# A four-layer image network on one core: begin stages of the last layer let in earlier, measured durations for the list scheduler, one softplus table load, and an accumulation walked by rows

## The chip, the core and the metric

The kernel runs as one program on one core of a Trainium2 chip. The core has a matrix engine (PE, with its weight loads shown as PEld), a vector engine (DVE), a scalar engine for activation functions (ACT), a general engine (POOL) and an engine that issues DMA transfers (SP). Each works through its own queue in order, and they wait for each other on semaphores. The metric is the device time of the whole program in microseconds (us), lower is better.

## The reference

Four layers are applied to four images of 192 channels and 56 x 56 pixels, all in fp32: layer 0 is a windowed aggregation with a learned 7x7 kernel per pixel and an MLP; layer 1 scales channels by a frequency gate; layer 2 is overlapped window attention, a gated 3x3 depthwise convolution and an MLP with a second depthwise convolution; layer 3 is a selective scan in four directions. The change touches layers 2 and 3. Layer 3 in short:

```python
xn = layer_norm(x)                       # over channels
xc, z = split(in_proj @ xn)
u = silu(depthwise3x3(xc) + conv_b)
for k in (rows, columns, rows reversed, columns reversed):
    dt, B, C = split(x_proj[k] @ u)      # 12, 4 and 4 channels
    dt = softplus(dt_proj[k] @ dt + b[k])
    h[l] = exp(dt[l] * A) * h[l-1] + dt[l] * B[l] * u[l]   # 4 states per channel
    y += C[l] . h[l] + D[k] * u          # put back in pixel order
out = x + out_proj @ (layer_norm(y) * silu(z))
```

## The kernel before

The 192 channels lie as two halves of 96 partitions. An image is cut into 7 chunks of 448 pixels (8 rows of 56; for the column directions, 8 columns of 56).

**Who sets the order.** In layers 2 and 3 the order of the instructions on PE, DVE, ACT and POOL is made when the program is built, by a list scheduler (`Order`, L241 to L321). Each piece of work is a Python generator that yields, before an instruction, its engine, an estimated duration and the buffers it takes (`on_pe`, `on_dve`, `on_act`, `on_pool`, `on_sp`, L324 to L346), or a condition that must hold first (`yield lambda: ...`). Each generator is added with a *place*. At every step, among the first 130 generators by place, the one with the lowest estimated start plus 0.05 us per unit of place goes next. Estimated durations therefore decide the order, not only gates and places; they have no effect on the chip beyond that. `on_dve` bills 0.08 us plus 1.05 ns an element. When an activation needs another function table than the scheduler has noted, the scheduler emits a table load itself (L315). If the named set is not the one that the activation is built to use, the compiler adds another load before the activation.

**Layer 2** (L1077 to L1673). `dwconv` (L1333 to L1343) does both depthwise convolutions on DVE, nine taps of one instruction per part.

**Layer 3** (L1676 to L2139). The scan of one image has 28 steps: rows, columns, columns reversed, rows reversed, with 7 chunks each. A step `t` is done in two *half steps*, one per channel half, so an image has 56 and the layer 224. Places count half steps: `scan(t, h)` has place 2t+h. Its parts:

- `begin(b, c)` (L1792 to L1879), an image's first stages for one chunk: load of x (L1803), the channel norm (`layer_norm`, L1763 to L1790: matmuls at L1768 and L1783, DVE at L1770 and L1789), the input projection (L1821), the depthwise convolution as 18 matmuls with diagonal weights (L1851), activations into `u` and the gate, the store of the gate, and `product` for the row directions (L1893), whose result goes to DRAM (L1899).
- `begin_columns(b, c)` (L1881 to L1885): the same product with `u` read column by column; it needs the row stage of all seven chunks.
- `load` (L1954), `sizes` (L1975): bring a step's products back and make `dt` (PE at L1985, softplus on ACT at L1997), two steps at a time.
- `decay` (L2012): spreads `dt` over the states by DMA (L2023) and takes exponentials on ACT (L2031).
- `scan` (L2034): `du` on DVE (L2046, L2049), replication on PE (L2056), multiply by B and scan on DVE (L2062, L2078), multiply by C on POOL (L2085), sum over states on PE (L2101), and the addition into `y` on DVE (L2106 for the first direction, L2111 for the last, L2114 for the two column directions).
- `final(b, c)` (L1902 to L1947): output norm, gate, projection (L1929) and store.

Two `u` tensors exist, so images b and b+1 may be in work at once. When `begin(b, c)` may start is set by L1800 (a gate on `multiplied`, the count of half steps whose replication has been issued), and its rank against other work by its place (L2127); L2128 ranks the column products.

Of the kernel before, what the change touches and what calls it, by code (L numbers as in the profile page):

```python
# [21 lines left out]
HALF = 96  # L22
# [301 lines left out]
def on_pe(n, *takes, ready=None):  # L324

    return "PE", 0.0019 * n, takes, None, ready


def on_dve(*n, takes=(), ready=None):
    return "DVE", sum(0.08 + 0.00105 * i for i in n), takes, None, ready  # L330


def on_scan(n, ready):
# [7 lines left out]
def on_pool(*n, each=0.0011):  # L341
    return "POOL", sum(0.2 + each * i for i in n), (), None, None
# [4 lines left out]


EXP_LN, GELU = "natural_log_exp_and_others", "gelu_and_others"
SILU, SOFTPLUS = "silu_and_others", "softplus_and_others"  # L350


def layers01(tc, x_in, packs, aps, dst):
# [723 lines left out]
def layer2(tc, src, packs, aps, dst):  # L1077
# [12 lines left out]
    with ExitStack() as ctx:  # L1090
# [242 lines left out]
        def dwconv(parts):  # L1333


            for t in range(9):
                yield on_dve(*(n * W for _, _, _, n, _, _ in parts))
                for dst, pad, i, n, wt, bias in parts:
                    x = pad[:, i + t // 3 : i + t // 3 + n, t % 3 : t % 3 + W]
                    if t == 0:  # L1340
                        nc.vector.tensor_scalar(dst, x, wt[:, 0:1], bias, ALU.mult, ALU.add)
                    else:
                        nc.vector.scalar_tensor_tensor(dst, x, wt[:, t : t + 1], dst, ALU.mult, ALU.add)  # L1343
# [332 lines left out]
def layer3(tc, src, packs, aps, dst):  # L1676
# [8 lines left out]
    with ExitStack() as ctx:  # L1685
# [74 lines left out]
        def gone(*what):  # L1760
            return what in passed
# [30 lines left out]
        def begin(b, c):  # L1792
# [4 lines left out]
            yield lambda: (b, c) == (0, 0) or (gone("begun", b, c - 1) if c else gone("begun", b - 1, NCHUNK - 1))  # L1797
            yield lambda: b < 2 or gone("scanned", b - 2)

            yield lambda: b == 0 or gone("multiplied", 8 * NSC * (b - 1) + 6 * c)  # L1800
            yield on_sp("row", "row")
            xl, xn = take("row"), take("row")
            nc.sync.dma_start(xl[:HALF], pixels(src[b])[:, :, c * CH : (c + 1) * CH])  # L1803
# [71 lines left out]
            yield on_sp()  # L1875
            nc.sync.dma_start(pixels(zmem[b])[:, :, c * CH : (c + 1) * CH], zt)
            done(zt)
            yield from product(b, 0, px, u[:, :, px])
            passed.add(("rows", b, c))  # L1879

        def begin_columns(b, c):  # L1881
            yield lambda: all(gone("rows", b, i) for i in range(NCHUNK))
            uv = us[b % 2].rearrange("p h (y x) -> p h x y", x=W)[:, :, 8 * c : 8 * c + 8]
            yield from product(b, 1, slice(c * CH, (c + 1) * CH), uv)
            passed.add(("columns", b, c))  # L1885

        def product(b, o, px, u):

            n = px.stop - px.start
            yield on_pe(2 * n, "bank")  # L1890
            pp = take()
            for k in range(2):
                nc.tensor.matmul(pp[:40, :n], w["c128.xpT"][:, k, o], u[:, k], start=(k == 0), stop=(k == 1))  # L1893
            yield on_act(n, takes=("prod",))
            t = take("prod")
            nc.scalar.copy(t[:, :n], pp[:40, :n])
            done(pp)
            yield on_sp()
            nc.sync.dma_start(prods[b][o][:, px], t[:, :n])  # L1899
            done(t)  # L1900
# [133 lines left out]
        def scan(t, h):  # L2034
# [5 lines left out]
            px = slice(c * SCH, (c + 1) * SCH)  # L2040
            yield lambda: t in sized and (2 * t + h == 0 or gone("multiplied", 2 * t + h - 1))
            dts, b_, c_ = sized[t]
            yield on_dve(SCH, takes=("du",))
            du = take("du")
            if o == 0:
                nc.vector.tensor_mul(du, dts[h], u[:HALF, h, px])  # L2046
# [20 lines left out]
            for j in range(3):  # L2067
                g = 3 * h + j
                yield lambda: (t, h, j) in decays and (head or (t - 1, g) in states)
                da, at = decays.pop((t, h, j))  # L2070
                yield on_scan(SCH, ready=max(at, ends[j]))
                sts.append(take("st"))
                r = slice(None, None, -1 if s else 1)
                first = 0.0
                if not head:
                    before = states.pop((t - 1, g))
                    first = before[:, 0:1] if s else before[:, SCH - 1 : SCH]
                nc.vector.tensor_tensor_scan(  # L2078
                    sts[j][:, r], da[:, r], tiles[j][:, :SCH][:, r], first, ALU.mult, ALU.add
                )  # L2080
                done(tiles[j])
                if not head:
                    done(before)
                yield on_pool(SCH, each=0.0021)
                nc.gpsimd.tensor_mul(da, sts[j], c_)  # L2085
                das.append(da)
                if last:
                    done(sts[j])
                else:
                    states[t, g] = sts[j]  # L2090
# [14 lines left out]
            if (o, s) == (0, 0):  # L2105
                nc.vector.scalar_tensor_tensor(  # L2106
                    y[:HALF, h, px], u[:HALF, h, px], d_sum[:, h : h + 1], sums, ALU.mult, ALU.add
                )
                started.add((t, h))
            elif o == 0:  # L2110
                nc.vector.tensor_add(y[:HALF, h, px], y[:HALF, h, px], sums)  # L2111
            else:
                yv = y[:HALF, h].rearrange("p (y x) -> p x y", x=W)[:, 8 * c : 8 * c + 8]
                nc.vector.tensor_add(yv, yv, rows2(sums, H))  # L2114
            done(py)
            added[b] += 1
            if o == 0 and s == 1 and h == 1:
# [6 lines left out]
        n = 8 * NSC  # L2124
        for b in range(B):
            for c in range(NCHUNK):
                order.add(n * (b - 1) + 6 * c + 24, begin(b, c))  # L2127
                order.add(n * (b - 1) + 44 + c, begin_columns(b, c))  # L2128
                order.add(n * (b + 1) - 2 * c, final(b, c))
        for t in range(len(steps)):  # L2130
            order.add(2 * t - 5, load(t))
# [40 lines left out]
```

## Time and profile before

| | us |
|---|---|
| median of 3 runs (lowest to highest) | 7017.2 (7013.4 to 7018.1) |
| the profiled execution | 7014.4 |
| its span, first to last instruction | 7012.6 |
| layers 0 and 1 | 0 to 2969 |
| layer 2 | 2969 to 4909 |
| layer 3 | 4909 to 7013 |

| busy over the span | PE | DVE | ACT | POOL |
|---|---|---|---|---|
| us | 5931.5 | 5950.0 | 2699.1 | 1408.0 |
| share | 85% | 85% | 38% | 20% |

The layers' borders are the times at which the next layer's packed weights are fetched (L219). A group of instructions is shown as line, engine, operation, output<-inputs, shapes, count, then busy us and the mean ns of one, then the idle time of its engine just before and what ended most of it. PE's busy time is modelled and overlaps where small matmuls run side by side, so a share below 100% can be a full PE. A wait "X <- Y" means that X's engine stood idle until Y was done. In the tables by stretch of time, each engine has busy us and the number of instructions; then come the granted PE clock as a share of full speed, the share of DMA time and GB/s.

### The profile page before, as it was taken

Reading aid. Unit: us, or ns where it says so; the run is one execution under the profiler, and the core shown is the slowest. Engines: PE = TensorE matmul, PEld = TensorE weight load, DVE = VectorE, ACT = ScalarE, POOL = GpSimd, SP = SyncE. Lnnn points to the kernel's source line nnn. Section 1 sums busy time; section 2 is a strip of 40 time slices with the busy share of each in tenths; the row PEclk is TensorE's granted clock in tenths of the full one; section 3 lists DMA queues with packets and bytes.
Section 4 is the critical chain, followed back from the end, with each engine's and each line's share of the span. In section 5 each row is a group of like instructions: output and inputs, shape, how many; then the busy total and the mean of one; then the engine's idle time right before and its main releaser. Section 6 shows DMA issues by size and latency. Waiting matters only on the chain.

```text
span 7012.6 us, 107574 instructions
## 1 busy us (share of the span) xinstructions
PE 5931.5 (85%) x43810; PEld 2703.5 (39%) x43810; DVE 5950.0 (85%) x7379; ACT 2699.1 (38%) x4134; POOL 1408.0 (20%) x1409
## 2 busy tenths in 40 slices
PE   4999989999999994877888888875888999888856
PEld 2444444444544441344444454442322322222212
DVE  2799999999999999548999989997269779698697
ACT  1111111222212221144455555553356666566544
POOL 0000000000000000032222122210235445355354
PEclk9999989999999997989999999997999999999977
DMA  3222112221222112210000000000246555465454
GB/s 93 56 52 68 31 32 60 52 68 29 63 51 66 35 43 70 64 32 16 17 20 15 19 16 19 18 13 7 60 116 152 135 130 147 115 151 147 118 131 112
DMA packets 252043, 462.68 MB, mean 66 GB/s; under 512 B 30388, under 2 KB 237964, under 8 KB 240412
## 3 DMA queue, kind: packets, MB, share of 16 engines
q1 hardware_dynamic: 251548, 455.80, 25.6%
q8 instruction: 345, 5.65, 0.3%
q14 instruction: 150, 1.23, 0.1%
HBM read 238.58 MB, written 62.96 MB: 43 GB/s over the span
## 4 chain that ended last, share of the span: by engine, by line
DVE 47%; PE 36%; issue 7%; ACT 5%; POOL 2%; DMA 2%; SPq 0%; DVEq 0%; POOLq 0%; ACTq 0%
DVE pr L789 9%; DVE oa L794 6%; PE a_bank L634 5%; DVE bg L1343 5%; PE c_bank L1851 4%; DVE ob L794 4%; DVE st L2078 3%; DVE bxn L1343 3%; PE c_bank L2056 2%; PE a_bank L884 2%; PE a_bank L869 2%; PE c_bank L1893 2%; PE c_bank L2101 2%; DVE c_bank L2062 2%; PE c_bank L1929 2%
## 5 line engine op out<-in xcount | busy, mean ns | idle before, releaser
L789 DVE TENSOR_TENSOR pr<-vdx,attn 112x1792 f32<-112x1792 f32 (+4 forms) x720 | 1185.9, 1649 | 19.0
L634 PE MATMUL a_bank<-qk_in,w_a 64*49 64x392 f32 x9408 | 1158.6, 496 | 0.0
L2085 POOL TENSOR_TENSOR da<-st,bc 128x448 f32<-128x448 f32 x672 | 845.4, 1267 | 884.9 <-DVE st L2078 793.7
L794 DVE TENSOR_TENSOR oa<-oa,pr 112x1792 f32<-112x1792 f32 (+1 forms) x423 | 765.1, 1809 | 0.0
L634 PE MATMUL a_bank<-qk_in,wd 64*49 64x392 f32 x4032 | 694.6, 496 | 0.0
L2078 DVE TENSOR_TENSOR_SCAN st<-da,st,c_bank 128x448 f32<-128x448 f32 x576 | 644.7, 1133 | 20.9 <-issue 12.7
L634 PEld LDWEIGHTS a_bank<-qk_in,w_a 64*49 64x49 f32 x9408 | 431.7, 120 | 395.9 <-issue 391.2
masks.py:197 POOL MEMSET b_ident<- 128x128 f32 x1 | 0.2, 206 | 2861.2 <-DVE sc L1042 2861.2
L2031 ACT ACTIVATE da<-da,a_neg 128x448 f32<-128x448 f32 x672 | 407.4, 658 | 155.8 <-DMA da<-dt 144.6
L315 ACT ACT_TABLE_LOAD x358 | 459.3, 1283 | 6.2
L2062 DVE TENSOR_TENSOR c_bank<-c_bank,bc 128x448 f32<-128x448 f32 x672 | 385.3, 619 | 75.3 <-PE c_bank L2056 74.5
L2056 PE MATMUL c_bank<-du,w_c 32*128 32x448 f32 x1344 | 291.3, 663 | 173.9 <-DVE du L2049 96.4
L1343 DVE SCALAR_TENSOR_TENSOR bg<-bzpad,w_b,bg 128x448 f32<-128x448 f32 (+2 forms) x672 | 421.8, 682 | 0.0
L1851 PE MATMUL c_bank<-pad,diag 128*96 128x448 f32 (+2 forms) x1008 | 413.0, 549 | 2.4 <-ACT pad L1832 2.4
L2101 PE MATMUL c_bank<-da,w_c 128*32 128x448 f32 x1344 | 343.8, 612 | 73.9 <-POOL da L2085 60.3
L794 DVE TENSOR_TENSOR ob<-ob,pr 112x1792 f32<-112x1792 f32 (+3 forms) x282 | 393.3, 1395 | 0.0
L869 PE MATMUL a_bank<-xc,w_a 128*128 128x448 f32 x672 | 300.8, 577 | 70.2 <-DVE xc L854 70.2
L878 ACT ACTIVATE hm<-a_bank,w_a 128x448 f32<-128x448 f32 x168 | 106.4, 634 | 644.9 <-PE a_bank L869 619.1
L634 PEld LDWEIGHTS a_bank<-qk_in,wd 64*49 64x49 f32 x4032 | 249.1, 120 | 256.4 <-issue 254.5
L1432 PE MATMUL bank<-bxn,w_b 128*128 128x448 f32 (+2 forms) x672 | 295.0, 567 | 16.7 <-DVE bxn L1215 16.3
L884 PE MATMUL a_bank<-hm,w_a 128*96 128x448 f32 x672 | 289.3, 562 | 21.1 <-ACT hm L878 21.1
L586 ACT ACTIVATE qk_in<-a_bank,qk_bias,qk_scale 64x224 f32<-64x224 f32 (+5 forms) x288 | 146.3, 526 | 412.2 <-PE a_bank L571 409.9
(306 smaller groups left out, 10091.6 us busy)
## 6 DMA issues: line engine op xcount, KB each, us to landing
da<-dt SPq DMA_DIRECT2D x672, 224.0 KB
vdx<-vmem SPq DMA_DIRECT2D x168, 476.0 KB
bc<-prod SPq DMA_DIRECT2D x224, 224.0 KB
row<-x SPq DMA_DIRECT2D x56, 336.0 KB
x<-x SPq DMA_DIRECT2D x4, 2352.0 KB
vmem<-vt SPq DMA_DIRECT2D x56, 168.0 KB
xc<-x SPq DMA_DIRECT2D x56, 168.0 KB
mid<-xc SPq DMA_DIRECT2D x56, 168.0 KB
```

Source lines behind the costliest of these rows:

```text
L315: self.nc.scalar.preload_act_table_set(table)
L634: nc.tensor.matmul(py[a][outs[g], : 7 * W].rearrange("p (y x) -> p y x", x=W), wt[halves[a], dx], q[halves[a], r, i0 + m : i0 + m + 7, dx ...
L789: nc.vector.tensor_mul(pr, vv, wt)
L794: nc.vector.tensor_add(og, og, before)
L869: nc.tensor.matmul(ph[:, :CH], w["a128.c1T"][:, k, 128 * m : 128 * m + 128], xt[:, k], start=(k == 0), stop=(k == 1),)
L1343: nc.vector.scalar_tensor_tensor(dst, x, wt[:, t : t + 1], dst, ALU.mult, ALU.add)
L1851: nc.tensor.matmul(rows2(pc[:HALF, : n * W]), diag[:, h, t], pad[:, h, at + t // 3 : at + t // 3 + n, t % 3 : t % 3 + W], start=(t == 0), ...
L2056: nc.tensor.matmul(tiles[j][:, :SCH], w["c96.rep"][r], du[r], start=True, stop=True)
L2062: nc.vector.tensor_mul(tiles[j][:, :SCH], tiles[j][:, :SCH], b_)
L2078: nc.vector.tensor_tensor_scan(sts[j][:, r], da[:, r], tiles[j][:, :SCH][:, r], first, ALU.mult, ALU.add)
L2085: nc.gpsimd.tensor_mul(da, sts[j], c_)
L2101: nc.tensor.matmul(py[32 * j : 32 * j + 32, :SCH], w["c128.sum"], das[j], start=True, stop=True)
```

## The change

There are six edits.

- The gate of `begin(b, c)` asks for 4c instead of 6c half steps of the image before, and its place falls from 6c + 24 to 6c + 4, counted from that image's first half step. The column products' place rises from 44 + c to 48 + c.
- Some estimated durations are replaced: the taps of layer 2 (1.2 ns an element instead of 1.05), `du` (1.5 or 1.8 instead of 1.05), POOL's multiply by C (2.4 instead of 2.1), and the column products (billed as four passes instead of two).
- The name of the softplus table set becomes `softplus`.
- The addition of the column directions' sums into `y` walks y row by row in runs of 8 pixels, and the sums in PSUM with a step of 56, where before it walked y with a step of 56 and the sums in order.

Nothing that is computed changes.

```diff
--- before.py
+++ after.py
@@ -326,8 +326,8 @@
     return "PE", 0.0019 * n, takes, None, ready
 
 
-def on_dve(*n, takes=(), ready=None):
-    return "DVE", sum(0.08 + 0.00105 * i for i in n), takes, None, ready
+def on_dve(*n, takes=(), ready=None, each=0.00105):
+    return "DVE", sum(0.08 + each * i for i in n), takes, None, ready
 
 
 def on_scan(n, ready):
@@ -347,7 +347,7 @@
 
 
 EXP_LN, GELU = "natural_log_exp_and_others", "gelu_and_others"
-SILU, SOFTPLUS = "silu_and_others", "softplus_and_others"
+SILU, SOFTPLUS = "silu_and_others", "softplus"
 
 
 def layers01(tc, x_in, packs, aps, dst):
@@ -1334,7 +1334,7 @@
 
 
             for t in range(9):
-                yield on_dve(*(n * W for _, _, _, n, _, _ in parts))
+                yield on_dve(*(n * W for _, _, _, n, _, _ in parts), each=0.0012)
                 for dst, pad, i, n, wt, bias in parts:
                     x = pad[:, i + t // 3 : i + t // 3 + n, t % 3 : t % 3 + W]
                     if t == 0:
@@ -1797,7 +1797,7 @@
             yield lambda: (b, c) == (0, 0) or (gone("begun", b, c - 1) if c else gone("begun", b - 1, NCHUNK - 1))
             yield lambda: b < 2 or gone("scanned", b - 2)
 
-            yield lambda: b == 0 or gone("multiplied", 8 * NSC * (b - 1) + 6 * c)
+            yield lambda: b == 0 or gone("multiplied", 8 * NSC * (b - 1) + 4 * c)
             yield on_sp("row", "row")
             xl, xn = take("row"), take("row")
             nc.sync.dma_start(xl[:HALF], pixels(src[b])[:, :, c * CH : (c + 1) * CH])
@@ -1875,19 +1875,19 @@
             yield on_sp()
             nc.sync.dma_start(pixels(zmem[b])[:, :, c * CH : (c + 1) * CH], zt)
             done(zt)
-            yield from product(b, 0, px, u[:, :, px])
+            yield from product(b, 0, px, u[:, :, px], 2)
             passed.add(("rows", b, c))
 
         def begin_columns(b, c):
             yield lambda: all(gone("rows", b, i) for i in range(NCHUNK))
             uv = us[b % 2].rearrange("p h (y x) -> p h x y", x=W)[:, :, 8 * c : 8 * c + 8]
-            yield from product(b, 1, slice(c * CH, (c + 1) * CH), uv)
+            yield from product(b, 1, slice(c * CH, (c + 1) * CH), uv, 4)
             passed.add(("columns", b, c))
 
-        def product(b, o, px, u):
+        def product(b, o, px, u, passes):
 
             n = px.stop - px.start
-            yield on_pe(2 * n, "bank")
+            yield on_pe(passes * n, "bank")
             pp = take()
             for k in range(2):
                 nc.tensor.matmul(pp[:40, :n], w["c128.xpT"][:, k, o], u[:, k], start=(k == 0), stop=(k == 1))
@@ -2040,7 +2040,7 @@
             px = slice(c * SCH, (c + 1) * SCH)
             yield lambda: t in sized and (2 * t + h == 0 or gone("multiplied", 2 * t + h - 1))
             dts, b_, c_ = sized[t]
-            yield on_dve(SCH, takes=("du",))
+            yield on_dve(SCH, takes=("du",), each=0.0018 if o else 0.0015)
             du = take("du")
             if o == 0:
                 nc.vector.tensor_mul(du, dts[h], u[:HALF, h, px])
@@ -2081,7 +2081,7 @@
                 done(tiles[j])
                 if not head:
                     done(before)
-                yield on_pool(SCH, each=0.0021)
+                yield on_pool(SCH, each=0.0024)
                 nc.gpsimd.tensor_mul(da, sts[j], c_)
                 das.append(da)
                 if last:
@@ -2110,8 +2110,9 @@
             elif o == 0:
                 nc.vector.tensor_add(y[:HALF, h, px], y[:HALF, h, px], sums)
             else:
-                yv = y[:HALF, h].rearrange("p (y x) -> p x y", x=W)[:, 8 * c : 8 * c + 8]
-                nc.vector.tensor_add(yv, yv, rows2(sums, H))
+
+                yv = y[:HALF, h].rearrange("p (y x) -> p y x", x=W)[:, :, 8 * c : 8 * c + 8]
+                nc.vector.tensor_add(yv, yv, sums.rearrange("p (x y) -> p y x", y=H))
             done(py)
             added[b] += 1
             if o == 0 and s == 1 and h == 1:
@@ -2124,8 +2125,8 @@
         n = 8 * NSC
         for b in range(B):
             for c in range(NCHUNK):
-                order.add(n * (b - 1) + 6 * c + 24, begin(b, c))
-                order.add(n * (b - 1) + 44 + c, begin_columns(b, c))
+                order.add(n * (b - 1) + 6 * c + 4, begin(b, c))
+                order.add(n * (b - 1) + 48 + c, begin_columns(b, c))
                 order.add(n * (b + 1) - 2 * c, final(b, c))
         for t in range(len(steps)):
             order.add(2 * t - 5, load(t))
```

## The prediction

> **What bounds the kernel now.** I read the page first, then the busy table by layer, the groups and waits of the last layer, and the timeline at the places where its scans stand still. Layers 0 and 1 end at 2969 us (the weights of layer 2 are fetched then), layer 2 at 4909. Columns: time, busy us (and instructions) of PE, PEld, DVE, ACT, POOL, then clock, DMA share, GB/s.
>
> ```profile
> 2969.00:4909.00 1940.00, 1516.69 (x15012) 868.31 (x15012) 1663.71 (x3261) 942.13 (x1414) 453.87 (x621) 0.89 0.07 19
> 4909.00:7013.00 2104.00, 1772.17 (x5504) 549.94 (x5504) 1595.99 (x1983) 1183.00 (x1659) 940.88 (x776) 0.91 0.49 126
> ```
>
> In the last layer neither DVE (76%) nor PE (84%, ends modelled) is full: they bound it in turn. Its unit is the half step: 3 scans on DVE, 224 of them (672 scans), 56 per image. From the starts of the scans, image 1's half step 0 is at 5562 us; 8 is at 5659, 47 at 5929, 55 at 6035, and half steps 7 and 8 of image 2 at 6105 and 6141. The busy table of these four stretches, and of half steps 8 to 47 of the last image, which has no next image to begin:
>
> ```profile
> 5659.00:5929.00 270.00, 238.49 (x813) 72.41 (x812) 256.69 (x320) 179.27 (x254) 150.88 (x125) 0.94 0.61 152
> 5929.00:6035.00 106.00, 98.54 (x302) 34.92 (x300) 69.52 (x88) 66.56 (x94) 39.10 (x32) 0.95 0.50 135
> 6035.00:6105.00 70.00, 59.90 (x194) 19.68 (x194) 56.52 (x72) 36.88 (x51) 33.43 (x31) 0.95 0.40 106
> 6105.00:6141.00 36.00, 33.42 (x69) 6.63 (x68) 10.47 (x15) 13.17 (x20) 3.48 (x4) 0.99 0.35 96
> 6628.00:6906.00 278.00, 177.68 (x548) 41.94 (x549) 252.57 (x310) 139.81 (x198) 156.97 (x118) 0.74 0.55 136
> ```
>
> The period is 270+106+70+36 = 482 us. In the first stretch DVE is full: 6.9 us per half step. In the rest DVE has 137 us of work in 212 and waits for PE. The timeline shows the worst wait, image 1's half step 7 (DVE, then PE):
>
> ```profile
> 5627.77 1.05 DVE L1770 TENSOR_TENSOR row<-row,c_bank 96x896 f32<-96x896 f32 x1
> 5651.76 0.68 DVE L2106 SCALAR_TENSOR_TENSOR y<-u,d_sum,c_bank 96x448 f32<-96x448 f32 x1 [22.94 <-PE c_bank L2101]
> ```
> ```profile
> 5607.48 7.85 PE L1851 MATMUL c_bank<-pad,diag 128*96 128x504 f32 x18
> ...
> 5624.81 24.97 PE L1893 MATMUL c_bank<-u,w_c 128*40 128x504 f32 x32
> ```
>
> PE has just finished the last chunk's convolution (L1851) and runs its row product and all seven column products (L1893) as one 25 us block in front of the sums (L2101) that DVE needs.
>
> **What the Trainium skill says.** TensorE: Matmul & The Clock Gate, HAM clock gate: the PE clock halves when PE has been idle for some 3.4 us and returns under load. The trace agrees: clock 0.74 where PE is lightest, 0.94 to 0.99 where it is dense, so packing PE work tighter shouldn't slow it. SBUF — State Buffer, Door 1: a stride past a 16-byte line costs bandwidth, while 8 neighbouring fp32 values don't; PSUM lines are 8 bytes. The first half agrees:
>
> ```profile
> L2114 DVE TENSOR_TENSOR y<-y,c_bank x112: 949/982/1015, 5228.5 to 6873.8; 96x448 f32<-96x448 f32 x112
> L2111 DVE TENSOR_TENSOR y<-y,c_bank x56: 587/609/618, 5423.7 to 6982.4; 96x448 f32<-96x448 f32 x56
> ```
>
> The same add costs 0.37 us more with y stepped by one image row (L2114), and layer 2's adds over runs of 8 (L1655: 256 elements, 409 ns) cost no extra. No DVE read of PSUM with a large step is in the trace. ScalarE: Activation LUTs, What ACT_TABLE_LOAD costs: 1283 ns for every set; the trace has exactly that.
>
> ```profile
> L315 ACT ACT_TABLE_LOAD x186 | 238.6, 1283 | 3.3
> L1997 ACT ACT_TABLE_LOAD x71 | 91.1, 1283 | 4.0 <-DVE st L2078 3.6
> ```
>
> **The change, part by part.**
>
> *Softplus table.* All 71 softplus batches load twice, at L315 and again at L1997. Naming the right set removes 71 x 1.283 = 91 us of ACT. In the changed program softplus batches rise to 81 and returns to the exp set from 87 to 99: 22 x 1.283 = 28 us back; layer 2 has 2 loads fewer. Net 65 us off ACT, which is busy 56% of the layer and hidden behind DVE and PE. DVE waits for softplus itself only 20.8 us (5 times). Value 0 to -20; I take -5.
>
> *y by rows.* 112 adds. With runs of 8 in y free, they fall to 0.61 us (-42 us on DVE). If the stepped PSUM read costs what stepped SBUF costs, 0; if shorter lines make it dearer, I allow the same 42 us the other way. I take 0.67 us, -35 us of DVE, of which what counts is where DVE is the bound. It is inside the tally below: -20 there, +25 at the bad end.
>
> *Durations.* Instructions and DMAs stay the same in kind; their order moves. In layer 2 the taps' cost goes from 0.55 to 0.62 us (trace: 0.68). Both programs have the same DVE instructions there, and the running sum of DVE work ahead of every tail chunk stays within 14 us of before, the last one equal. Layer 2 keeps DVE 86% busy, so its cover is thin: 0 +-15. POOL's multiply, billed at 1.14 us against 1.27 measured, is now billed at 1.28, so sums are placed when POOL is done; PE weight loads wait 234 us for POOL at L2101 now. A part of that stands before DVE waits: -5 to -15, I take -10. On SP's queue each chunk's row load, z store, row-product store and column-product store move with it, past the decay copies (`da<-dt`), which wait behind them when a row buffer is late; ACT's exponentials wait 145 us for those copies now and hide it, no wait of DVE in the loop names a DMA, and DMA is 0.4 to 0.6 busy. On POOL a chunk's pad copies (0.37 us) move past the multiplies; POOL is 45% busy. Value 0.
>
> *Earlier begin and spread columns.* This is the main part. In the program before, the convolutions of an image's seven chunks stand after half steps 11, 20, 27, 39, 48 and 55 of the image before and 5 of its own, with eight products in one place after that. In the changed one they stand after 5 or 6, 11, 17, 23, 28, 35 and 40 of the image before, and the seven column products at about one per half step from 44 to 48. The gate at four (24 for the last chunk) is not what binds; chunks follow each other 5 to 7 half steps apart.
>
> I sum PE's work between the `rep` matmuls (L2056) of consecutive half steps. Spacings from the timeline at full clock: L1851, L1821, L1768, L1783, L1929 and row products 0.376 us a record (18 convolution records in 6.77 us), two records a matmul; three concurrent L2056 pairs 0.94; three L2101 pairs 0.86; L1985 pair 0.46; column products 0.78 a record. Divided by the clock of 0.95, each half step costs the larger of this and its DVE work (scan 1.10, multiply 0.57, du 0.80 or 0.95, add 0.62 or 0.93, norms 1.05, final add 0.58, net of overlap). Check on before: the four stretches come out as 278, 107, 71, 31 against 270, 106, 70, 36: the gaps of 15.4, 18.5, 28.2 and 29.3 us of PE work at half steps 47, 48, 54 and 63 are its stalls. The last stretch is 5 us short: the chain product, copy, DMA, softplus, decay, scan.
>
> Changed: PE's total per image stays 359 us at full clock, but no gap is over 14.9: 10.9, 10.9+11.9, 12.4, 14.0, 13.9, 13.4, 14.9 and two about 11. There are 20 gaps above 8 us instead of 10, each cut by only 7 us of DVE work. By the strict larger-of rule the layer from half step 0 on goes from 1915 to 1889 us: middle images 487 to 479, the last 439 to 403, image 0 503 to 528, since it now carries all of image 1's beginning. But DVE has up to two scans and an add (3 us) left after the next du, so PE may lead by up to 3 us; granted in full, 1847 to 1804. Middle of -26 and -43: -35. The boundary chain of 5 us now ends half an image early: three times, -14.
>
> Sum: -35 -14 -10 -5 +0 = -64 us against the profiled execution's own 7014.4 us (span 7012.6): 6950. The median of the runs is 2.8 us above that execution: 6953.
>
> **Rivals.** *Fully pooled*, 15%: if PE's gaps average out over a stretch, a middle image costs 40+269+47+57 = 413 us, all DVE. 3 x (482-413) = -207, image 0 some +20: near 6830. For it: half steps 8 to 47 now run at DVE's pace with gaps to 8.7. Against: no stall over 15 us was pooled at all. *Strict*, 20%: no lead, and the PSUM step costs what y's did: -5 -14 -5, near 6990; a rest of this case lies within 0.2%. *Not what it says: PE becomes the bound*, 12%: half steps 5 to 43 hold seven beginnings, 252 us of PE at clock 0.95 beside 269 of DVE. PE's queue is in order; if inside each of the ten gaps above 10 us a sum or a normalisation isn't ready and PE stands 4 us more, with no lead, a middle image costs 479+40 = 519: +111 over three, less 36 in the last: near 7090. It decides from about 2 us per gap on top of my case. Against: in the new order normalisation, variance and projection stand one or two half steps apart.
>
> **How the numbers follow.** My case has 53%, its own range 6915 to 6985. Pooled 15%, strict 20% (8 of it within 0.2%), bound by PE 12%. The range cuts most of the pooled case and the slow one: 6875 to 7020. Faster by over 0.2% (14 us, what this measurement can tell): 53+15+12 = 80%; within: 8%; slower: 12%.
>
> **What would show it.** The last layer near 2040 us, layer 2 within 15 of 1940. No scan gap near 35 us; column products in seven pieces of 3.1 us. L2114's successor at 0.6 to 0.7 us (wrong at 0.9). Table loads 380 in all, none at the softplus line. Half steps 5 to 43 of a middle image in 300 to 325 us, clearly slower than 6.9 each; 43 to 61 near DVE's pace. I am wrong if that first stretch takes under 280 or over 345 us, or if layer 2 moves by over 20.

## The result, and the profile after

The changed kernel takes 6955.1 us (median of 5 runs, 6949.4 to 6961.7) against 7017.2 for the kernel before on the same chip: a ratio of 0.9912, with a 95% interval of 0.9898 to 0.9927. The prediction was 6953. The total is right; the terms of the sum are only partly so, as the runs below show.

The profiled execution spans 6949.9 us, 62.7 less than before. Layers 0 and 1 end at 2964 us, layer 2 at 4902. The busy table of layers 2 and 3 (columns as in the prediction: time, busy us and instructions of PE, PEld, DVE, ACT, POOL, clock, DMA share, GB/s):

```profile
2964.00:4902.00 1938.00, 1504.40 (x15012) 865.51 (x15012) 1670.81 (x3260) 940.80 (x1412) 456.68 (x621) 0.89 0.07 19
4902.00:6950.00 2048.00, 1744.80 (x5504) 535.45 (x5504) 1547.91 (x1983) 1125.71 (x1610) 953.91 (x776) 0.94 0.51 130
```

Layers 0 and 1 give 5 us; their code is the same, and over the profiles of this study they end anywhere from 2964 to 2973. Layer 2 gives 2. The last layer gives 56. It would be natural to read that off DVE's column: DVE's work in the last layer fell from 1596 to 1548 us, by 48, most of it y's 112 adds. That reading is wrong, as the run that puts y back will show. The starts of the scans show where the time went; "end" is the last instruction, and half step 47 to the end is called the tail:

| last layer, us | before | after |
|---|---|---|
| start to half step 0 of image 0 | 162.5 | 167.1 |
| image 0 | 491.0 | 516.9 |
| image 1 | 481.2 | 475.5 |
| image 2 | 484.3 | 466.8 |
| image 3 to the end | 484.8 | 421.8 |
| of it half steps 0 to 8, 8 to 47, 47 to the end | 99.8, 278.7, 106.3 | 58.5, 243.0, 120.3 |

Image 0 pays 26 us for carrying all of image 1's beginning. The two middle images give back 23 between them. How much each of them gives can't be said: a kernel with the same order in this layer ("The taps", below) has 466.8 and 475.3 us where this one has 475.5 and 466.8, so a single image is known to no better than 9 us, though the two together repeat to 0.2. The last image, which has no next one to begin, gives 63: 41 at its border (half steps 0 to 8), 36 in its long stretch of plain scanning, and it loses 14 in its tail.

Three stretches of the kernel after in the busy table: half steps 5 to 43 of image 1, where the seven beginnings of image 2 now stand; from there to half step 5 of image 2, where the columns stand; and half steps 8 to 47 of the last image.

```profile
5640.00:5945.00 305.00, 281.02 (x933) 89.48 (x932) 243.22 (x315) 185.55 (x263) 151.44 (x125) 0.97 0.54 132
5945.00:6114.00 169.00, 141.45 (x439) 40.94 (x438) 137.05 (x176) 97.23 (x142) 80.22 (x66) 0.91 0.57 150
6587.00:6830.00 243.00, 174.02 (x556) 37.73 (x556) 237.99 (x315) 121.87 (x180) 155.81 (x118) 0.93 0.58 151
```

The first is bound by PE (281 of 305, DVE 243). The last is the surprise: its instructions are those of before (118 multiplies on POOL in both, 315 DVE instructions against 310), DVE has 15 us less to do, and yet it takes 35 us less, at a granted clock of 0.93 where before had 0.74. Of the 35, 15 are DVE's work and 20 its idle time, which falls from 25 to 5 us. This stretch is called the light stretch below.

The border of an image, about half step 7 of image 2, on DVE's timeline (start us, us, engine, line, operation, output<-inputs, count, then the idle time before it and its releaser):

```profile
6126.63 1.14 DVE L2078 TENSOR_TENSOR_SCAN st<-da,st,c_bank 128x448 f32<-128x448 f32 x1
6127.68 1.66 DVE L2062 TENSOR_TENSOR c_bank<-c_bank,bc 128x448 f32<-128x448 f32 x3
...
6131.89 0.65 DVE L2106 SCALAR_TENSOR_TENSOR y<-u,d_sum,c_bank 96x448 f32<-96x448 f32 x1
```

Before, L2106 stood 22.94 us behind PE at such a place; here it doesn't stand at all. From the first half steps of image 0 on there is no spacing of scans over 16 us (the longest ones there: 15.8), where before each border had one of 35 to 38 and each image but the last one of 29. But PE's debt to DVE was cut up rather than paid. What DVE waited for in the last layer, us in total, times and longest, before and then after:

```profile
DVE y L2106 <- PE c_bank L2101: 134.0, 25, 24.1
...
DVE c_bank L2062 <- PE c_bank L2056: 74.5, 76, 8.0
...
DVE y L2114 <- PE c_bank L2101: 12.6, 20, 1.5
```
```profile
DVE c_bank L2062 <- PE c_bank L2056: 152.5, 95, 10.5
...
DVE y L2115 <- PE c_bank L2101: 93.5, 29, 6.0
...
DVE y L2106 <- PE c_bank L2101: 60.6, 19, 17.8
```

The waits at L2106 lose 73 us, those at L2062 and at the column adds gain 159. The other waits lose some 94; the largest part is the norm's wait for ACT at L1789, which falls from 71.1 to 33.5. DVE's whole idle time in the layer is 2104 - 1596 = 508 us before and 2048 - 1548 = 500 after. Two smaller edits read directly off their rows:

```profile
L2115 DVE TENSOR_TENSOR y<-y,c_bank x112: 581/612/622, 5239.0 to 6800.1; 96x448 f32<-96x448 f32 x112
L2111 DVE TENSOR_TENSOR y<-y,c_bank x56: 585/607/618, 5473.0 to 6926.9; 96x448 f32<-96x448 f32 x56
```
```profile
L315 ACT ACT_TABLE_LOAD x378 | 485.0, 1283 | 6.6
```

The column add (L2115, was L2114) costs what the row add costs (L2111, a control that didn't change). Table loads are 378 at the scheduler's line and two elsewhere, none at the softplus line.

### The profile page after: what moved, and what is told of

Same layout as the page of the kernel before. It is cut to its first block, busy times and chain, and to the rows that moved or that the text cites. A ratio compares the mean times of both kernels' runs of the same rounds, so it can differ in the third digit from the quotient of the medians.

```text
span 6949.9 us, 107660 instructions
## 1 busy us (share of the span) xinstructions
PE 5890.7 (85%) x43810; PEld 2685.0 (39%) x43810; DVE 5908.5 (85%) x7379; ACT 2640.6 (38%) x4083; POOL 1423.8 (20%) x1409
## 5 line engine op out<-in xcount | busy, mean ns | idle before, releaser
L2062 DVE TENSOR_TENSOR c_bank<-c_bank,bc 128x448 f32<-128x448 f32 x672 | 382.5, 618 | 153.1 <-PE c_bank L2056 152.5
L2101 PE MATMUL c_bank<-da,w_c 128*32 128x448 f32 x1344 | 349.5, 570 | 66.3 <-POOL da L2085 61.4
L1851 PE MATMUL c_bank<-pad,diag 128*96 128x448 f32 (+2 forms) x1008 | 396.8, 543 | 2.4 <-ACT pad L1832 2.3
L2056 PE MATMUL c_bank<-du,w_c 32*128 32x448 f32 x1344 | 257.8, 624 | 121.6 <-DVE du L2046 80.4
L655 PE MATMUL a_bank<-qk_sum,w_a 64*49 64x168 f32 (+1 forms) x5376 | 277.7, 337 | 27.1 <-DVE qk_sum L625 25.2
```

The costliest lines, as they stand in the source:

```text
L1851: nc.tensor.matmul(rows2(pc[:HALF, : n * W]), diag[:, h, t], pad[:, h, at + t // 3 : at + t // 3 + n, t % 3 : t % 3 + W], start=(t == 0), ...
L2056: nc.tensor.matmul(tiles[j][:, :SCH], w["c96.rep"][r], du[r], start=True, stop=True)
L2062: nc.vector.tensor_mul(tiles[j][:, :SCH], tiles[j][:, :SCH], b_)
L2101: nc.tensor.matmul(py[32 * j : 32 * j + 32, :SCH], w["c128.sum"], das[j], start=True, stop=True)
```

## The experiments

Differences between runs are given as differences of their ratios to the kernel before, times 7017 us, since the kernel before itself moved by 4 us between the sets of runs. An interval is about 0.0015 of a ratio, 10 us, to each side, so a difference of two ratios is sure from about 14 us on (an estimate from these intervals). The last layer by itself is a second measure, from one profile of each kernel: with the same order it took 2048.2 and 2045.8 us. "The tally" is the prediction's sum of PE's and DVE's work per half step. The single edits undone from the changed kernel come first.

### y as it was

```diff
-                yv = y[:HALF, h].rearrange("p (y x) -> p y x", x=W)[:, :, 8 * c : 8 * c + 8]
-                nc.vector.tensor_add(yv, yv, sums.rearrange("p (x y) -> p y x", y=H))
+                yv = y[:HALF, h].rearrange("p (y x) -> p x y", x=W)[:, 8 * c : 8 * c + 8]
+                nc.vector.tensor_add(yv, yv, rows2(sums, H))
```

> The changed kernel with the column addition walking y by columns again; order of all instructions unchanged. Theory A (the tally per half step): 112 adds cost 0.37 us more, 42 us of DVE, and about 25 of them fall where DVE is the bound: 6955 + 25 = 6980 us, most of it in the last image (half steps 8 to 47 from 243 to about 254 us). Rival B (the y edit is what made the last image's pace faster, by keeping DVE ahead of PE): the whole 35 us of that stretch come back, 6990 to 7000 us. Rival C (DVE is never the bound): 6955 us.

Measured 6972.5 us (6970.6 to 6976.1), ratio 0.9935 (0.9922 to 0.9949): y is worth 16 us, where about 25 was expected. Half steps 8 to 47 of the last image go from 243.0 to 253.9 us, 10.9 for 28 column adds of 0.37 us each (10.4), with no loss on the way. Images 0 to 2 together move by 3.7. The last layer of this kernel:

```profile
4905.00:6967.00 2062.00, 1753.31 (x5508) 534.81 (x5506) 1589.08 (x1987) 1125.60 (x1610) 954.62 (x777) 0.94 0.51 129
```

DVE has 41 us more to do and the layer is 14 longer: where the next image is being begun, PE is the bound and DVE's saving falls into idle time. So y's 41 us of DVE work explain 14 to 16 of the change's 62, not most of them.

### The old table name

```diff
-SILU, SOFTPLUS = "silu_and_others", "softplus"
+SILU, SOFTPLUS = "silu_and_others", "softplus_and_others"
```

> The changed kernel with the old name of the softplus set; order unchanged, 81 table loads more (461 instead of 380), 104 us of ACT. Theory A: ACT is covered, +5 us: 6960 us, at most 6975. Rival (the softplus chain paces the scans where PE is light, and the single load is what made the last image faster): 30 to 60 us slower, 6985 to 7015 us, with half steps 8 to 47 of the last image back above 260 us.

Measured 6960.1 (6959.3 to 6963.2), ratio 0.9918 (0.9904 to 0.9931): 4 us, as large as expected and not told apart from nothing. The 81 double loads are back, 104 us of ACT, and the light stretch stays at 243.1 us.

```profile
L1997 ACT ACT_TABLE_LOAD x81 | 103.9, 1283 | 4.8 <-DVE st L2078 4.3
```

### The old gate and places

```diff
-            yield lambda: b == 0 or gone("multiplied", 8 * NSC * (b - 1) + 4 * c)
+            yield lambda: b == 0 or gone("multiplied", 8 * NSC * (b - 1) + 6 * c)
-                order.add(n * (b - 1) + 6 * c + 4, begin(b, c))
-                order.add(n * (b - 1) + 48 + c, begin_columns(b, c))
+                order.add(n * (b - 1) + 6 * c + 24, begin(b, c))
+                order.add(n * (b - 1) + 44 + c, begin_columns(b, c))
```

> The changed kernel with gate 6c and places 6c+24 and 44+c again; durations, table and y as changed. Theory A (moving the first stages is the main part): the tally of PE work between half steps gives +21 to +27, and the wait of some 35 us at each image's half step 7 comes back with its chain (+14): about 6993 us, and the last image again takes some 60 us more from its half step 0 on. Rival B (the durations carry it): within 10 us of 6955. Rival C (all of it is the places): back to 7017.

Measured 6991.8 (6990.2 to 6998.1), ratio 0.9964 (0.9952 to 0.9977): the places are worth 37 us on top of the rest. In the profiles the last layer takes 2077.0 us instead of 2048.2, 29 more; the rest of that execution's difference stands before it, where the order is the same. The stall at the border is back with them. On DVE at half step 7 of image 1:

```profile
5630.64 1.06 DVE L1770 TENSOR_TENSOR row<-row,c_bank 96x896 f32<-96x896 f32 x1
5654.58 0.68 DVE L2106 SCALAR_TENSOR_TENSOR y<-u,d_sum,c_bank 96x448 f32<-96x448 f32 x1 [22.88 <-PE c_bank L2101]
```

Image 0 takes 488.4 us (28 less than after), images 1 and 2 take 481.3 each, and half steps 0 to 8 of the last image 102.0 instead of 58.5. (Its light stretch is 12 us longer too, and its tail 16 shorter.) This is the mechanism of the prediction: the block is taken apart at every border, its work is paid for in the image before, and the last image's border is free.

### The old durations in the last layer

```diff
-            yield from product(b, 1, slice(c * CH, (c + 1) * CH), uv, 4)
+            yield from product(b, 1, slice(c * CH, (c + 1) * CH), uv, 2)
-            yield on_dve(SCH, takes=("du",), each=0.0018 if o else 0.0015)
+            yield on_dve(SCH, takes=("du",))
-                yield on_pool(SCH, each=0.0024)
+                yield on_pool(SCH, each=0.0021)
```

> The changed kernel with layer 3's old estimated durations (du, POOL's multiply, column products); gate, places, table, y and layer 2's taps as changed. Theory A as it was predicted: 10 us slower, 6965. The tally of the built order says more: the blocks of PE work stand otherwise, 35 us slower: 6990 us, all of it in images 0 to 2. Rival (the durations don't matter): 6955 us within 5.

Measured 7015.2 (7010.6 to 7019.2), ratio 0.9993 (0.9985 to 1.0001): a miss, both values too low. Without four numbers that the chip never sees, nothing of the gain is left, places, y and table notwithstanding. They are worth 57 us, where the prediction had 10. The clearest place is again half steps 8 to 47 of the last image, where no next image is begun:

```profile
6633.00:6905.00 272.00, 184.03 (x563) 42.59 (x563) 245.20 (x317) 122.30 (x182) 157.10 (x119) 0.72 0.55 136
```

The same instructions as after, 272 us instead of 243, clock 0.72 instead of 0.93. Two theories then stood. One, from the prediction's own term: POOL's bill, through the sums that are placed before POOL is done. The other (D): `du`, billed at 0.55 us (0.08 + 448 x 1.05 ns), takes 0.60 us by median in the row directions and 0.98 in the column ones, so the scheduler believes that the replication can go earlier than it can, and lays PE's queue out wrongly. (The means before, with the slow ones told of at the end, are 0.86 and 1.01; the new bills come to 0.75 and 0.89.) The next two runs undo one bill each.

### POOL's bill alone, and du's bill alone

```diff
-                yield on_pool(SCH, each=0.0024)
+                yield on_pool(SCH, each=0.0021)
```

> The changed kernel with POOL's multiply billed at 2.1 ns an element again, nothing else. Theory D (the durations work through du: with du billed right, every half step has its own replication and its own sums on PE, so PE never stands idle for 6 us in the light stretches and keeps its clock): the light order keeps its pattern here, so half steps 8 to 47 of the last image stay at 243 to 248 us with a clock above 0.9; the tally of the built order gives +5 to +13 us: about 6965 us. Theory P (POOL's bill is what counts, because PE otherwise stands in front of sums that POOL has not finished): most of the 60 us come back, 6995 to 7015 us.

```diff
-            yield on_dve(SCH, takes=("du",), each=0.0018 if o else 0.0015)
+            yield on_dve(SCH, takes=("du",))
```

> The changed kernel with du billed at 1.05 ns an element again, nothing else. In the built order two of every four half steps of the light stretches have their replications one behind the other and six sums after them. Theory D: PE idles some 6 us before every fourth replication there, its clock falls to about 0.75, half steps 8 to 47 of the last image take 265 to 272 us, and the time is 7000 to 7015 us. Theory P: 6955 to 6970 us and that stretch at 243.

Without POOL's new bill the kernel takes 6939.1 (6937.3 to 6946.9), ratio 0.9887 (0.9872 to 0.9902): it is 17 us *faster* than the changed one (in the profiles' last layers 2031.0 against 2048.2). Without `du`'s new bill it takes 7007.9 (7002.4 to 7014.5), ratio 0.9984 (0.9977 to 0.9990): 50 of the 57 us are gone. So `du` it is, and POOL's bill, the one that the prediction counted on, costs time. Both expectations missed POOL's run in the total: one had 6965, the other 6995 or more. What the one for `du` said of the light stretch held: 245 us at a clock of 0.92 without POOL's bill, 275 (expected 265 to 272) at 0.75 without `du`'s. Which of `du`'s two new numbers does it was not tried. By difference some 24 us would fall to the columns' bill, which wasn't undone alone; as the parts don't add (below), that is no measurement of it.

How one bill does it shows on PE's timeline in that stretch. With `du` billed short:

```profile
6718.61 1.87 PE L2056 MATMUL c_bank<-du,w_c 32*128 32x448 f32 x6 [7.11 <-DVE du L2049]
6720.41 3.21 PE L2101 MATMUL c_bank<-da,w_c 128*32 128x448 f32 x12
6727.47 1.87 PE L2056 MATMUL c_bank<-du,w_c 32*128 32x448 f32 x6 [3.85 <-DVE du L2049]
6729.27 2.14 PE L2101 MATMUL c_bank<-da,w_c 128*32 128x448 f32 x6
6731.34 1.00 PE L1985 MATMUL c_bank<-dr,w_c 64*96 64x448 f32 x4
6733.04 1.03 PE L2056 MATMUL c_bank<-du,w_c 32*128 32x448 f32 x6 [0.71 <-DVE du L2049]
```

and in the changed kernel:

```profile
6724.18 1.87 PE L2056 MATMUL c_bank<-du,w_c 32*128 32x448 f32 x6
6725.98 3.64 PE L2101 MATMUL c_bank<-da,w_c 128*32 128x448 f32 x6
6730.22 1.03 PE L2056 MATMUL c_bank<-du,w_c 32*128 32x448 f32 x6 [0.59 <-DVE du L2049]
6731.23 0.94 PE L2101 MATMUL c_bank<-da,w_c 128*32 128x448 f32 x2
6733.02 0.94 PE L2101 MATMUL c_bank<-da,w_c 128*32 128x448 f32 x2 [0.85 <-POOL da L2085]
6734.59 0.94 PE L2101 MATMUL c_bank<-da,w_c 128*32 128x448 f32 x2 [0.63 <-POOL da L2085]
6735.46 1.00 PE L1985 MATMUL c_bank<-dr,w_c 64*96 64x448 f32 x4
6736.38 1.03 PE L2056 MATMUL c_bank<-du,w_c 32*128 32x448 f32 x6
```

In the first, the sums of two half steps (12 records of L2101) come in one lump, and PE stands 7.1 and 3.9 us until the next `du` is there; behind both pauses L2056's six records take 1.87 us instead of 1.03, and DVE waits for them. In the second, one half step's sums stand between two replications, and no pause shown is over 0.9 us; the longest of the whole stretch is 3.0. A slow replication occurs here too (1.87 us at 6724.18), but it is rare: 6 of 39 take over 1.3 us, with 1.1 us of DVE's waits behind them, where with `du` billed short 18 of 39 do, 15 of these right behind a pause of over 3.4 us, with 15.0 us of waits. Over the stretch, by the groups of PE (idle time in front, and what ended it), `du` billed short and then the changed kernel:

```profile
L2056 PE MATMUL c_bank<-du,w_c 32*128 32x448 f32 x234 | 54.5, 771 | 102.0 <-DVE du L2049 85.2 <-DVE du L2046 15.2 <-ACT da L2031 1.5
```
```profile
L2056 PE MATMUL c_bank<-du,w_c 32*128 32x448 f32 x234 | 44.2, 640 | 22.7 <-DVE du L2049 15.3 <-DVE du L2046 6.8 <-ACT da L2031 0.5
```

PE's pauses of over 3.4 us, counted between its matmul records in half steps 8 to 47 of the last image:

| kernel | pauses over 3.4 us | clock | us |
|---|---|---|---|
| before | 8 | 0.74 | 278.7 |
| `du` billed as before | 15 | 0.75 | 275.4 |
| the durations as before | 7 | 0.72 | 271.7 |
| gate and places as before | 1 | 0.83 | 255.1 |
| y as before | 0 | 0.88 | 253.9 |
| after | 0 | 0.93 | 243.0 |
| POOL billed as before | 0 | 0.92 | 245.0 |
| the places alone (below) | 7 | 0.78 | 273.2 |
| the durations alone (below) | 1 | 0.82 | 267.0 |

Three kernels here besides the one before have its `y` add, 10 us of the stretch: y as before and the two last. A low clock is not in itself the loss. With y as before it is 0.88 instead of 0.93, in the same order, yet DVE idles 5 us in both. With `du` billed short the 32 us are 17 of waits for the replications, 9 of waits for the sums and 6 of longer DVE work.

What POOL's bill costs stands in the tail. With the bill undone, the last half steps and the closing norm and projection (47 to the end) take 105 us instead of 120, at a clock of 0.88 instead of 0.80; the light stretch is 2 us longer, and the other images differ by +5, -5 and +1. The long tail belongs to this one order rather than to a wrong bill: POOL's new bill of 1.28 us is what the multiply takes (1.28 by mean), and the tail is also 104 to 105 us with a bill between the two or with the old gate (both below). In the changed kernel's tail DVE stands where it didn't have to:

```profile
6853.88 0.62 DVE L2111 TENSOR_TENSOR y<-y,c_bank 96x448 f32<-96x448 f32 x1 [4.43 <-PE c_bank L2101]
```

### Either half alone, on the kernel before

The places alone are the diff above, the other way round; the durations alone are the four last-layer bills without layer 2's taps. Both start from the kernel before, with its y and its table name.

> The kernel before with the gate at 4c and the places 6c+4 and 48+c, and nothing else of the change. If the edits add up: 7017 - 37 = 6980 us. From undoing the durations (60 us) with y (17) and table (5) on top: 7037 us, slower than before. The tally of the built order says the same sign: 15 to 34 us slower, less 14 for the boundary chains. I expect 7020 to 7040.

> The kernel before with layer 3's measured durations (du, POOL's multiply, column products) and nothing else of the change. If the edits add up: 7017 - 60 = 6957 us. From undoing the places (37 us) with y (17) and table (5) on top: about 7014 us, no change; half steps 8 to 47 of the last image still fall from 279 to about 265, and the waits at the image borders eat the rest.

The places alone take 7031.1 (7021.6 to 7038.3), ratio 1.0014 (1.0005 to 1.0022): slower by 10, as expected. The durations alone take 7038.8 (7032.7 to 7041.1), ratio 1.0024 (1.0015 to 1.0034): slower by 17, where about no change was expected (7014 us), a clear miss. Both together, with y and table, are faster by 62. So the parts don't add: undone one at a time they are worth 16, 4, 37 and 57 us, 114 in all (by the last layers of the profiles 14, 4, 29 and 56, some 102 in all, against 56).

The images show half of why. The places alone move work from the last image (484.8 to 439.0) to the first (491.0 to 535.0), but the light stretch stays at 273.2 us, for `du` is billed short, and each middle image is 7 to 10 us longer. The durations alone quicken the light stretch (278.7 to 267.0) but leave the block at the border, whose stall grows from 35 to 40 us. Why images 0 to 2 then take 7 to 11 us more each, when the changed kernel with old places has 488 and 481, isn't settled by these runs; that kernel also has the new y and table.

### The taps, the gate, and POOL's bill between

```diff
-                yield on_dve(*(n * W for _, _, _, n, _, _ in parts), each=0.0012)
+                yield on_dve(*(n * W for _, _, _, n, _, _ in parts))
```

> The changed kernel with layer 2's taps billed at 1.05 ns an element again; the last layer's order unchanged. Theory: layer 2 moves by less than 5 us (1937 us now) and the time is 6955 within 5. Rival: the taps' cost is worth 10 us or more in layer 2, 6965 us or above.

Measured 6952.2 (6951.2 to 6953.9), ratio 0.9905 (0.9890 to 0.9919): no difference. Layer 2 takes 1937.8 us against 1937.5. The order of the last layer is that of the changed kernel on all four engines, so this run also shows what repeats there: the last layer took 2.4 us less.

```diff
-            yield lambda: b == 0 or gone("multiplied", 8 * NSC * (b - 1) + 4 * c)
+            yield lambda: b == 0 or gone("multiplied", 8 * NSC * (b - 1) + 6 * c)
```

> The changed kernel with the gate of begin at 6c again and the new places kept. The prediction said that the gate is not what binds. If so: 6955 us within 5. But the built order is another one, and the tally of PE work between half steps gives +11 to +17 us for it: 6966 to 6972 us.

Measured 6965.5 (6964.8 to 6970.4), ratio 0.9923 (0.9906 to 0.9939): slower by 8, less than the tally's 11 to 17, and within the intervals. A gate of six does bind, for the order changes: half steps 5 to 43 of image 1 take 324.5 us instead of 305.7, and 43 to 61 take 153.4 instead of 169.2. Images 0 to 2 are 8, 2 and 11 us longer, the tail 17 shorter (103.5), the last layer in all 4 longer; the rest of this execution's difference lies in the earlier layers, whose code is the same.

```diff
-                yield on_pool(SCH, each=0.0024)
+                yield on_pool(SCH, each=0.0022)
```

> The changed kernel with POOL's multiply billed at 2.2 ns an element, between the old 2.1 (6939 us) and the new 2.4 (6955 us). Theory S (a bill only decides which of many orders is built, and its nearness to the measured 1.27 us says nothing): the tally of this order is 22 to 25 us below that of 2.1, so about 6916 us. Rival (the bill acts smoothly): between 6939 and 6955 us.

Measured 6951.1 (6950.0 to 6956.8), ratio 0.9904 (0.9890 to 0.9919): a miss of 35 us by the tally, and inside the range of the rival, a bill that acts smoothly. The parts are no blend, though: the tail is 104.7 us as with POOL's old bill, while images 0 and 1 are as in the changed kernel. The tally, which gives an order its time from PE's and DVE's work alone, ranked these bills wrongly.

### Chunks five half steps apart

The last run combines what was learnt: POOL's bill as before, and begin places of 5c + 12, so that the beginnings are spread from later on and closer together.

```diff
-                yield on_pool(SCH, each=0.0024)
+                yield on_pool(SCH, each=0.0021)
-                order.add(n * (b - 1) + 6 * c + 4, begin(b, c))
+                order.add(n * (b - 1) + 5 * c + 12, begin(b, c))
```

> The changed kernel with begin's place at 5c + 12 and POOL billed at 2.1 ns an element. By the tally of PE work between half steps this order is 17 to 29 us shorter than the same with 6c + 4 (6939 us): about 6916 us. If the tally is no guide among orders this close: 6939 us or more.

Measured 6910.9 (6907.7 to 6915.4), ratio 0.9846 (0.9831 to 0.9861), near the tally's value this time: 46 us less than the changed kernel, 29 less than with POOL's bill alone undone, and 108 less than the kernel before. Its last layer:

```profile
4908.00:6906.00 1998.00, 1721.26 (x5504) 524.27 (x5504) 1551.16 (x1986) 1122.04 (x1606) 952.68 (x777) 0.95 0.53 133
```

DVE's work is the same (1551 against 1548 us); it idles 447 us instead of 500. Against POOL's bill alone undone, images 0 to 2 take 511.8, 460.4 and 448.7 us instead of 521.6, 470.2 and 467.6, and the last 408.6 instead of 404.4: the gain is in the middle of the layer, and half steps 5 to 43 of image 1 take 300.2 instead of 319.4.

## Why the prediction was right, and where it wasn't

*The main part, begin and columns: right.* The strict tally gave image 0 +25, the two middle images -16 together and the last one -36; measured +26, -23 and -63. The last one gained 27 more than the tally, which leads to the term that failed. The places undone gave 37 us and brought the stall back at its old place with its old length. Half steps 5 to 43 took 306 us, inside the 300 to 325 named. The seven column products are six pieces, five of 3.5 us and one of 6.8, at PE's pace between half steps 43 and 48.

*y: right in kind and size.* The stepped read of PSUM costs next to nothing: 0.612 us against 0.607 in order, where 0.67 was taken. The tally's 20 us are 16. *Table: right*, 4 us against 5. *Layer 2: right*, 2 us and no effect of the taps. *Boundary chains, 14 us:* no run measured them apart; the last image's border, 41 us less, holds the stall and its chain together.

*Durations: the term that failed.* The prediction said "POOL's multiply, billed at 1.14 us against 1.27 measured, is now billed at 1.28, so sums are placed when POOL is done", and took -10. Undone, POOL's bill gains 17 us, and weight loads at L2101 wait for POOL 259 us in the changed kernel, against 234. The gain of the bills comes from `du`, 50 us, to which the prediction gave no term of its own. The reason lies in how the step was costed. The tally knows only the work of each half step and one clock of 0.95. It has no place for an order inside the half step, nor for a clock that depends on it. It was compared with the kernel before in a middle image only. For the last image its figure before, 439 us, is 46 short of the 484.8 measured, and the line shown for the light stretch read DVE 252.57 of 278 at a clock of 0.74: 25 idle us that no term explained.

The prediction quoted the Trainium skill, TensorE: Matmul & The Clock Gate, HAM clock gate, to argue that packing PE more tightly wouldn't slow it. The same sentence, read the other way, points to what was missing: the clock falls after about 3.4 us of idle PE, so an order that lets PE pause that long lowers it. The table of pauses agrees in part: 7 to 15 such pauses go with a clock of 0.72 to 0.78, one with 0.82 to 0.83, none with 0.88 to 0.93. But such a pause isn't needed: in the changed kernel the clock is 0.50 from 6723.4 to 6730.1 us, with no pause of over 2.1 us in the 7 us before. How much of the 32 us between `du`'s two bills is the clock and how much is the pause itself isn't told apart: no run held PE's order and idle time and changed only the clock. DVE's wait for the replications there, 21.7 us against 4.5, holds both, though 15.0 of the 21.7 stand at the slow replications.

*"The gate at four is not what binds": right.* Built with a gate of 3c, or of 0, the kernel comes out as the very same program. A gate of six does bind: put back, it lengthens the beginnings' stretch by 19 us and shortens the columns' by 16; of the sum, 4 us in the last layer's profile and 8 by the medians, no loss is sure. *Half steps 43 to 61 "near DVE's pace": wrong.* They take 9.4 us each with DVE 137 of 169 us busy; the places 5c + 12 bring them to 157.

*The total was right by luck, because errors met.* The sum added up the parts and took 10 us for the durations. Undone, the durations are worth 57, some 47 more, but the parts don't add: one by one they come to 114 us, together to 62, 52 less. The two about cancel. Nothing in the prediction foresaw that each half alone would be a loss. Whether PE leads DVE by up to 3 us, as the tally's middle value took it, no run shows.

## What to carry to other kernels

In a list-scheduled kernel an estimated duration is an edit of every queue: compare the bills with the measured means, those of the cheap instructions that release another engine first, and try each by itself, since one changed bill can help and the next one, billed just as measured, can hurt. Where an engine's clock is low in a stretch, list its pauses and what ends them before counting its work: the bound may be the order that causes the pauses, and not the busiest engine. When a change has parts that feed each other (work moved, and the estimates that place it), run them together as well as apart; a part that loses alone isn't therefore worthless.

## What the runs showed of the hardware

A DVE add that reads PSUM with a step of 56 fp32 values and y in runs of 8 takes 612 ns for 448 elements by 96 partitions, against 607 in order and 982 with y stepped by 56 and PSUM in order: only the stepped SBUF side cost anything. The same PE work, 231 matmul records of sums and 234 of replications, got a mean clock of 0.93 or 0.75 by its order alone, with 0 or 15 pauses over 3.4 us. In one and the same order it got 0.93 or 0.88, with 28 DVE adds of 0.61 us or 0.98 and no such pause. And `du` in the row directions (L2046), one multiply of 96 x 448, has two durations. Of 112, the 19 that overlap POOL's gate product in `final` (L1920, 96 x 896) take 1.5 to 2.6 us; the other 93 take at most 0.79. One of the 19, POOL and then DVE:

```profile
6841.68 2.07 POOL L1920 TENSOR_TENSOR row<-row,gate 96x896 f32<-96x896 f32 x1 [4.90 <-DMA bc<-prod]
6843.71 1.13 POOL L2085 TENSOR_TENSOR da<-st,bc 128x448 f32<-128x448 f32 x1
```
```profile
6842.72 2.60 DVE L2046 TENSOR_TENSOR du<-dt,u 96x448 f32<-96x448 f32 x1
```

`du` is issued while L1920 runs, and ends 0.5 us after the multiply behind it has ended (6844.84 to 6845.32): it lets both pass. Where `du` comes first, as it mostly does, it takes its 0.6 us and POOL's multiply, begun 0.2 us later, is drawn out to 1.4 us instead of 1.13. The Trainium skill, SBUF — State Buffer, SBUF: two separate sides, names the cause: DVE with two SBUF inputs and POOL share a pair of ports under "an exclusive lock", and whoever comes second waits out the other's whole instruction. The trace agrees in both directions; that the waiting `du` also lets a second POOL instruction pass is seen in it too. The 19 cost DVE 28 us over their usual 0.595 each, in the columns' stretches and the tail, where DVE isn't full; the kernel before has 15 such, all over 2 us, for 27. No run took the overlap away, so what it costs the end is open.
